# The last sort of a quantile graph layer: operation size and pauses in its DVE sorting network

## The chip, the cores and the metric

The kernel runs on one core of a Trainium2 chip. A core has a matrix engine (TensorE, PE in the profile), a vector engine (VectorE, DVE), a scalar engine (ScalarE, ACT), GpSimd (POOL) and a queue for plain DMAs (SyncE, SP). Each takes its instructions in the order in which they are written and waits for the others by semaphores. The metric is device time in microseconds. Before the change it is 1443.4 us, the median of three runs (1442.67 to 1445.76).

## The reference

For each of 16 graphs of 1024 nodes with 64 features, a layer does the following:

```
h   = max(layernorm(x), 0)
rem = every skip-th neighbour of a node with more than 10, made symmetric
nd  = (adjacency with self loops) without rem
for each node n and each feature c:
    s   = sorted values h[j, c] over the neighbours j of n in nd
    agg = 0.25 * quantile(s, 0.25) + 0.5 * quantile(s, 0.5) + 0.25 * quantile(s, 0.75)
out = h + agg
x   = x + mask * (relu(out @ W1 + b1) @ W2 + b2)
```

A quantile is interpolated between two neighbouring sorted values. The adjacency has about eight neighbours per node, so the lists are short, but they differ in length.

## The kernel before, in words

Two graphs form a pair, so there are eight pairs, m = 0 to 7. Within a graph the nodes are reordered by their number of neighbours and laid out as eight tiles of 128 nodes (tile 0 has the longest lists). For each node the kernel works out a list of neighbour indices. `fetch` (line 1319) then queues one indirect DMA for each slot of each tile and graph, issued by GpSimd at line 1332: it gathers, for 128 nodes, the 64 features of one neighbour into the tile `g`. There are 952 such gathers. In the last pair, `pick` (line 1373) brings some slots by one-hot matmuls instead.

Tiles are sorted in classes of equal slot count: tile 0 (13 slots), tiles 1 to 3 (11), tiles 4 and 5 (9), tiles 6 and 7 (7). The few longest lists of eight graphs are set apart and form a group of rows with a network of its own in the tile `gg` (`set_apart`, line 1483; `fetch_group`, line 1667; `aggregate_group`, line 1694). There are two groups; the second is treated next to the last pair.

`sort` (line 1417) runs a sorting network over the slots, found beforehand and written down in `PLANS`. Each step compares up to a few slots with as many others: a DVE minimum or maximum into a free slot (line 1440) and the opposite, in place (line 1445); a step of which one side only is needed has a single operation (line 1437). Afterwards the slots that can hold a quantile are scaled by their weights: by DVE at line 1462, or, in pairs from the sixth on (`by_act`), by ACT at line 1460, one slot and one node tile at a time. TensorE then sums the scaled slots into `acc` or `gacc` in PSUM (line 1466).

A flag `whole` of `sort` sets how long its operations are and what stands behind them:

```python
        most = max(1, (WHOLE if whole else PART) // size)
        gap = (lambda ins: ins) if whole else opened
```

`PART` is 384 and `WHOLE` is 1024 elements per partition. `size` is the width of one slot: 64 for the group, 128 for tile 0, 384 for tiles 1 to 3, and, in the last pair, 128 for the other two classes, since `aggregate` (line 1496) takes the two graphs of the last pair one after the other there. `opened` (line 856) puts behind an operation a DVE memset of one element of a scratch tile (line 859), called a pause here:

```python
        at = len(tails) % 64
        tails[nc.vector.memset(pause[:, at:at + 1], 0.0).ins.name] = ins.ins.name
        return ins
```

In pairs 0 to 6 and the first group, and in other long DVE operations such as the one-hot comparisons of lines 1392 and 1572, every operation has a pause. In the last pair (`last`) and the second group the sort has `whole` set.

The tail of the program, from about 1286 us, holds the sort of the second group, the MLP of pair 6 (`one_hot`, `sums`, `mlp`), the sort of tile 0, then of tiles 1 to 3, then, graph by graph, of tiles 4 to 7. Before some of these sorts ACT copies a few rows from one tile's slot to another's and DVE overwrites where they stood (lines 1528 and 1531). Results of the group's rows come back into the pair by `bring_back` (line 1726, tile `few`). The MLP of each graph of the last pair follows its sorts; it ends in lines 1615 to 1663.

The order of the instructions on each engine isn't that of the source. `arrange` (line 713) takes the whole list of instructions with their dependences and an assumed cost of each (`Step.cost`: a gather 1345 ns, a DVE operation by its elements, 12 ns more for a pause), plans it forwards and backwards six times, keeps the shortest plan and fixes that order on every engine. A gather may also wait for a DVE or ACT instruction that is planned to end 25 us before it (`LEASH`).

Of the kernel before, what the change touches and what calls it, by code (L numbers as in the profile page):

```python
# [70 lines left out]
GROUP = 8  # L71
# [481 lines left out]
ACTP, ACTB = 5, 13  # L553
# [115 lines left out]
def between(s, o):  # L669

    return s.lag + 60 if o.engine != s.engine or s.moves else 115 if s.engine == "DVE" else 0
# [141 lines left out]
def list_layer(  # L813
# [15 lines left out]
    B = x.shape[0]  # L829
# [489 lines left out]
    def fetch(m, classes=CLASSES, halves=(0, 1)):  # L1319

        for tiles, slots in classes:
            lo, n = tiles[0], len(tiles)
            held, order = PLANS[slots][:2]

            def begin(h, tiles=tiles, lo=lo, n=n, slots=slots, held=held):
                opening((tiles, slots), m)
                nc.scalar.copy(gathered[m, tiles][:, slots - 1, :, h], owns[m][:, lo:lo + n, h])

            issued, given_out = paced

            def gather(h, slot, k, at, tiles=tiles, lo=lo):
                ins = nc.gpsimd.indirect_dma_start(  # L1332
                    out=gathered[m, tiles][:, slot, k - lo, h], out_offset=None, in_=tables[2 * m + h][0],
                    in_offset=bass.IndirectOffsetOnAxis(ap=lists[2 * m + h][:, at:at + 1], axis=0),
                    element_offset=tables[2 * m + h][1], engine_sem=issued,
                )
                given_out[ins.ins.name] = ins
                return ins

            for h in halves:  # L1340
                queue.append(partial(begin, h))
                for k in tiles:
                    for s, slot in enumerate(order[:FULL[k] + ((k, FULL[k]) in HOSTS)]):
                        if m < pairs - 1 or s >= LEAST[k]:
                            queue.append(partial(gather, h, slot, k, PASSED[k] + s))
# [129 lines left out]
    def terms(acc, out):  # L1475

        for n in range(3):
            to = out[n]
            nc.scalar.copy(to, acc)
            if n < 2:  # L1480
                nc.tensor.matmul(acc, minus16, to, start=False, stop=True, skip_group_check=True)  # L1481
# [14 lines left out]
    def aggregate(m, o, between=None):  # L1496


        last = m == pairs - 1
        coef = coefs[m]  # L1500
        for half in (0, 1) if last else (1, 0):
            parts = CLASSES[2 * half:2 * half + 2][::1 if last else -1]
            for sides in ((0, 1), (1, 2)) if last and half else ((0, 2),):
                hs, one = slice(*sides), sides[0] if last and half else None
                if not one:
                    shape = [P, 4, 2, C] if one is None else [P, 2, 4, C]
                    tag, bufs = ("mx", 3) if last and not half else ("agg", 2)
                    whole = psum.tile(shape, F32, name="acc", tag=tag, bufs=bufs)
                    for tiles, slots in parts:
                        rows, own = slice(tiles[0] - 4 * half, tiles[-1] + 1 - 4 * half), gathered[m, tiles][:, slots - 1]  # L1510
                        nc.tensor.matmul(
                            whole[:, rows] if one is None else whole[:, :, rows], ident32,
                            own if one is None else own.rearrange("p n h c -> p h n c"),
                            start=((tiles, slots) == parts[0]), stop=False, skip_group_check=True,
                        )
                acc = whole if one is None else whole[:, one]
                if one is not None:
                    yield from between(one, False)
                line = {}
                for tiles, slots in parts:  # L1520
                    for k in tiles:
                        for s, slot in enumerate(PLANS[slots][1]):
                            line[k, s] = gathered[m, tiles][:, slot, k - tiles[0], hs]
                            if s >= FULL[k] and (k, s) not in HOSTS:
                                nc.vector.memset(line[k, s], BIG)
                for host, guest, first, stop in GUESTS:
                    if host in line:
                        nc.scalar.copy(line[guest][first:stop], line[host][first:stop])
                for host, lo, hi in BARE:
                    if host in line:  # L1530
                        nc.vector.memset(line[host][lo:hi], BIG)
                for tiles, slots in parts:
                    lo, n = tiles[0], len(tiles)
                    g = gathered[m, tiles]
                    plan = PLANS[slots]
                    if one is None:
                        lines, weigh = g.rearrange("p s n h c -> p s (n h c)"), partial(
                            lambda s, many, lo, n: coef[:, s:s + many, lo:lo + n].rearrange("p s n h -> p s (n h)"),
                            lo=lo, n=n,
                        )  # L1540
                    else:
                        lines, weigh = g[:, :, :, one], partial(
                            lambda s, many, lo, n, h: coef[:, s:s + many, lo:lo + n, h], lo=lo, n=n, h=one
                        )
                    yield from sort(
                        lines, plan, window(tiles, slots)[0], weigh, acc[:, lo - 4 * half:lo - 4 * half + n],
                        m >= ACTP, last,
                    )
                    if sides[1] == 2:
                        gathered.pop((m, tiles))  # L1550
                if half and not last:
                    for h in ((0, 1),) if m < pairs - 2 else ((0,), (1,)):
                        fetch(m + 1, CLASSES[2:], halves=h)
                terms(acc, [
                    o[:, 4 * half:4 * half + 4, hs if one is None else one, C * n:C * n + C] for n in range(3)
                ])
                if last and not half:
                    bring_back(m, o)
                if one is not None:
                    yield from between(one, True)  # L1560
# [133 lines left out]
    def aggregate_group(grp):  # L1694
        n = GROUP // 4
        gg = groups.pop(grp)
        to, xg = gathered.pop(("group", grp))
        coef = wk.tile([P, TOP, n], F32, name="gcoef", bufs=1)
        weights(coef, group_num[grp][:, :, 1], n, TOP)
        yield 1.0  # L1700
        tag, bufs = ("mx", 3) if grp == B // GROUP - 1 else ("agg", 2)
        acc = psum.tile([P, n, C], F32, name="gacc", tag=tag, bufs=bufs)
        nc.tensor.matmul(acc, ident32, gg[:, CAP - 1], start=True, stop=False, skip_group_check=True)
        for k in range(n)[::-1]:
            yield from sort(
                gg[:, :, k], PLANS[(CAP, SECOND + 1)[k]], window((0,), CAP)[0],
                lambda s, many: coef[:, s:s + many, k:k + 1], acc[:, k], whole=grp == B // GROUP - 1,
            )
        o = wk.tile([P, n * C], F32, name="go", tag="lows", bufs=1)
        nc.scalar.copy(o, acc.rearrange("p k c -> p (k c)"))  # L1710
        yield 0.0
        tp = psum.tile([P, P], F32, name="ot", tag="misc")
        nc.tensor.transpose(tp, o, ident32)
        ot = wk.tile([P, P], F32, name="got", tag="h1", bufs=1)
        nc.scalar.copy(ot, tp)
        yield 0.0
        h1 = wk.tile([P, n, P], F32, name="gh1", tag="highs", bufs=1)
        for k in range(n):
            hp = psum.tile([P, P], F32, name="hp", tag="misc")
            nc.tensor.matmul(hp, w1[k * C:(k + 1) * C], ot[k * C:(k + 1) * C], start=True, stop=True)  # L1720
            nc.scalar.activation(h1[:, k], hp, AF.Relu, bias=b1c)
            yield 0.0
        output(h1.rearrange("p k r -> p (k r)"), n, group_num.pop(grp)[:, :, 0], xg)
        gathered["out", grp], gathered["sum", grp] = (to, xg), o
# [143 lines left out]
def window(tiles, n):  # L1868

    return min(LEAST[k] for k in tiles) // 4, -(-3 * (n - 1) // 4) + 1  # L1870
# [176 lines left out]
```

## Time and profile before

| | |
|---|---|
| median of three runs | 1443.4 us |
| the profiled execution | 1448.98 us, span 1447.2 us |
| GpSimd busy | 1049.3 us, 73%; its 952 gathers 1013.1 us |
| DVE busy | 1220.1 us, 84% |
| PE busy | 1100.0 us, 76% |
| ACT busy | 1041.4 us, 72% |
| pauses on DVE (line 859) | 2043, the last at 1314.1 us |

The profile is of one execution. Its times are counted from the first instruction. A row of the timeline gives the start and the length in microseconds, the engine, the source line, the operation and its tiles (written<-read), and in brackets how long the engine sat idle before it and what is inferred to have ended that. Instructions of one engine overlap somewhat: a DVE operation's row ends a little after the next one has started, so its cost to the queue is read from start to start. [...]

### The profile page before, as it was taken

How to read it: one execution, taken by the hardware profiler on the slowest of the kernel's cores; microseconds unless marked ns; L12 is line 12 of the kernel's file. 1: busy time of each engine (PE TensorE's matmuls, PEld its weight loads, DVE VectorE, ACT ScalarE, POOL GpSimd, SP SyncE). 2: the span in 40 equal slices, each digit the busy share in tenths (PEclk: the TensorE clock that was granted, in tenths of full speed). 3: DMA queues.
4: the chain of work that ended last, by engine and by line, in shares of the span. 5: the costliest groups of instructions: out<-in, count | busy, mean ns of one | idle time of the engine just before them, and what ended most of it. 6: DMA issues, size and time to landing. Idle time of an engine off the chain costs nothing. (4 is left out here: it accounts for less than half of the span.)

```text
span 1818.2 us, 30222 instructions
## 1 busy us (share of the span) xinstructions
PE 1225.8 (67%) x8995; PEld 774.2 (43%) x9011; DVE 1225.1 (67%) x5869; ACT 1064.3 (59%) x2869; POOL 1028.3 (57%) x991
## 2 busy tenths in 40 slices
PE   6637576578777778567764886646774769623937
PEld 4425344344444445344442544434442446512524
DVE  5605287764786768775658768687657846786895
ACT  7646466567673868356661757363573775324865
POOL 0353565455555656654556565656556656677770
PEclk9759788798888898778887898777896889866958
DMA  5422232222231314121331213231220110112110
GB/s 193 133 77 84 86 96 73 70 68 77 78 112 47 102 37 136 44 74 47 92 98 38 77 44 117 48 94 34 58 72 21 33 24 22 21 25 48 35 26 14
DMA packets 128831, 121.67 MB, mean 67 GB/s; under 512 B 95730, under 2 KB 96274, under 8 KB 128658
## 3 DMA queue, kind: packets, MB, share of 16 engines
q1 hardware_dynamic: 97106, 87.29, 15.6%
q0 software_dynamic: 31552, 32.36, 8.1%
q8 instruction: 73, 1.20, 0.3%
q14 instruction: 100, 0.82, 0.1%
HBM read 108.79 MB, written 9.05 MB: 65 GB/s over the span
## 5 line engine op out<-in xcount | busy, mean ns | idle before, releaser
L1332 POOL DMA_INDIRECT g<-gtab,idx x952 | 991.6, 1042 | 733.5 <-issue 267.7
L1440 DVE TENSOR_TENSOR g<-g 128x384 f32<-128x384 f32 (+2 forms) x659 | 311.5, 493 | 21.6 <-ACT g L1413 7.4
L1445 DVE TENSOR_TENSOR g<-g 128x384 f32<-128x384 f32 (+2 forms) x659 | 310.7, 493 | 10.9 <-DMA gg<-g 6.0
L1145 PE MATMUL codeP<-pack,perm 128*128 128x332 bf16 x1024 | 201.0, 344 | 57.7 <-DVE perm L1120 38.6
L1048 ACT ACTIVATE dist<-rk,bias 128x512 f16<-128x512 f32 x256 | 168.2, 699 | 68.7 <-remote 25.6
L981 ACT ACTIVATE ne<-tp 128x512 fp8e4<-128x512 f32 x248 | 143.3, 610 | 101.4 <-remote 64.0
L1466 PE MATMUL acc<-g,kf 128*128 128x128 f32 (+2 forms) x472 | 148.5, 451 | 71.6 <-ACT g L1460 36.6
L1071 ACT ACTIVATE kept<-kp 128x512 fp8e4<-128x512 f32 x224 | 131.7, 601 | 87.5 <-PE kp L1066 41.8
L968 PE MATMUL tp<-kb,sg 128*128 128x128 bf16 x1024 | 117.7, 249 | 89.4 <-ACT dist L1048 34.2
L1145 PEld LDWEIGHTS <-perm 128*128 128x128 bf16 x1024 | 103.7, 108 | 149.4 <-DVE perm L1120 47.6
L1038 PE MATMUL rk<-kb,cnt 128*128 128x512 bf16 x256 | 114.1, 446 | 72.6 <-ACT dist L1048 38.6
L1043 PEld LDWEIGHTS <-ne 128*128 128x128 fp8e4 x1024 | 91.3, 110 | 132.4 <-issue 109.7
L968 PEld LDWEIGHTS <-sg 128*128 128x128 bf16 x1024 | 88.1, 113 | 127.0 <-issue 107.1
L1460 ACT ACTIVATE g<-g,coef 128x64 f32<-128x64 f32 x336 | 87.7, 341 | 77.0 <-DVE g L1440 65.0
L961 ACT ACTIVATE sg<-at 128x1024 bf16<-128x1024 f32 x122 | 130.6, 1071 | 3.0 <-DMA at<-in_adj_dram 2.8
L1466 PEld LDWEIGHTS acc<-g,kf 128*128 128x128 f32 x472 | 87.9, 225 | 102.8 <-ACT g L1460 46.1
L1049 DVE TENSOR_SCALAR rem<-dist,half 128x1024 bf16<-128x1024 f16 x128 | 62.9, 494 | 98.8 <-ACT dist L1048 88.2
L859 DVE MEMSET pause<- 128x1 bf16 x2043 | 120.5, 59 | 1.8 <-issue 1.8
L1158 ACT CAST st<-codeP 128x4 bf16<-128x4 f32 x128 | 20.7, 162 | 171.8 <-DVE rest L1156 87.3
L1043 PE MATMUL rk<-kw,ne 128*128 128x128 fp8e5 x1024 | 120.8, 245 | 0.0
L1061 PE MATMUL kp<-ne,kw 128*128 128x512 fp8e4 x256 | 108.5, 425 | 18.0 <-ACT kept L1071 9.6
L1066 PE MATMUL kp<-kw,rem 128*128 128x128 fp8e5 x1024 | 111.3, 234 | 0.0
(202 smaller groups left out, 2471.2 us busy)
## 6 DMA issues: line engine op xcount, KB each, us to landing
at<-in_adj_dram SPq DMA_DIRECT2D x122, 512.0 KB
g<-gtab,idx POOLq DMA_INDIRECT x952
xt<-in_x_dram SPq DMA_DIRECT2D x16, 256.0 KB
y<-in_x_dram SPq DMA_DIRECT2D x16, 256.0 KB
gtab<-xt SPq DMA_DIRECT2D x16, 256.0 KB
out_dram<-y SPq DMA_DIRECT2D x14, 256.0 KB
spare<-in_adj_dram SPq DMA_DIRECT2D x6, 512.0 KB
gg<-g SPq DMA_DIRECT2D x32, 48.0 KB
```

What stands on the lines that cost most here:

```text
L859: tails[nc.vector.memset(pause[:, at:at + 1], 0.0).ins.name] = ins.ins.name
L961: nc.scalar.activation(sg, at, AF.Sign)
L968: run.append(nc.tensor.matmul(tp[:, s], sg[:, m * P:(m + 1) * P], ident16, start=(s == 0), stop=(s == 3 and t // 4 != n), skip_group_check ...
L981: nc.scalar.activation(to, tp, AF.Relu, saturate=False)
L1043: run.append(nc.tensor.matmul(rk[:, s * P:(s + 1) * P], ne[:, 4 * n + s, ts], upper, start=False, stop=(s == 3), skip_group_check=True,))
L1048: nc.scalar.activation(dist[:, n * HALF:(n + 1) * HALF], rk, AF.Abs, bias=bias[:, t:t + 1])
L1071: nc.scalar.activation(kept[:, 4 * n:4 * n + 4], kp, AF.Relu, saturate=False)
L1145: run.append(nc.tensor.matmul(flat, perm[:, t, k * P:(k + 1) * P], pack[:, t], start=False, stop=(t == NT - 1), skip_group_check=True,))
L1332: ins = nc.gpsimd.indirect_dma_start(out=gathered[m, tiles][:, slot, k - lo, h], out_offset=None, in_=tables[2 * m + h][0], in_offset=bass ...
L1440: nc.vector.tensor_tensor(at(f + k * df, df, many), pa, pb, OP.min if what == "<" else OP.max)
L1445: nc.vector.tensor_tensor(pa if back else pb, pa, pb, OP.max if what == "<" else OP.min)
L1466: nc.tensor.matmul(acc, ident32, lines[:, s], start=False, stop=(s == now[-1] and not ends), skip_group_check=True)
```

## The change

The flag `whole` is off everywhere. The comparisons of the last pair and of the second group are therefore cut at 384 elements per partition instead of 1024, and each has a pause behind it, as in the pairs before. The order of all engines is worked out anew from the changed list.

```diff
                     yield from sort(
                         lines, plan, window(tiles, slots)[0], weigh, acc[:, lo - 4 * half:lo - 4 * half + n],
-                        m >= ACTP, last,
+                        m >= ACTP, False,
                     )
...
             yield from sort(
                 gg[:, :, k], PLANS[(CAP, SECOND + 1)[k]], window((0,), CAP)[0],
-                lambda s, many: coef[:, s:s + many, k:k + 1], acc[:, k], whole=grp == B // GROUP - 1,
+                lambda s, many: coef[:, s:s + many, k:k + 1], acc[:, k], whole=False,
             )
```

## The prediction

> **What bounds the kernel now.** I read the chain of waits first, for the end of the span:
>
> ```profile
> 1395.99 2.11 POOL g L1332
> ...
> 1398.41 3.84 POOL g L1332
> ...
> 1410.04 2.64 DMA g<-gtab,idx
> ...
> 1412.90 0.76 DVE g L1440 x2
> ...
> 1428.46 2.71 PE acc L1466 x24
> ```
>
> Columns: start, length, what. DVE's last sort (second batch of the last pair, slots of tiles 4 to 7) starts at 1412.9 because a gather issued at 1410.04 has only then landed. GpSimd (POOL) is the queue that is late. Its timeline over the tail shows why:
>
> ```profile
> 1271.02 0.94 POOL L1332 DMA_INDIRECT g<-gtab,idx  x1 [0.30 <-DMA g<-gtab,idx]
> ...
> 1280.28 1.19 POOL L1332 DMA_INDIRECT g<-gtab,idx  x1 [0.30 <-DMA g<-gtab,idx]
> ...
> 1332.45 5.14 POOL L1332 DMA_INDIRECT g<-gtab,idx  x1 [0.30 <-DMA g<-gtab,idx]
> ...
> 1372.01 8.20 POOL L1332 DMA_INDIRECT g<-gtab,idx  x1 [0.30 <-DVE gg L1440]
> 1380.51 0.94 POOL L1332 DMA_INDIRECT g<-gtab,idx  x1 [0.30 <-DMA g<-gtab,idx]
> ```
>
> The idle time before each gather is a constant 0.30 us, so the releasers named there cost nothing: the queue runs back to back, and only the length of a gather varies. Up to 1300 none is longer than 1.62 us; from 1317 on thirteen lie between 1.57 and 8.20. From the one at 1317.51 to the one at 1410.04 there are 50 steps in 92.5 us.
>
> What DVE did beside them is in its timeline:
>
> ```profile
> 1275.29 0.41 DVE L1445 TENSOR_TENSOR g<-g 128x256 f32<-128x256 f32 x1
> 1275.31 0.06 DVE L859 MEMSET pause<- 128x1 bf16 x1
> 1275.63 0.41 DVE L1440 TENSOR_TENSOR g<-g 128x256 f32<-128x256 f32 x1
> ...
> 1336.69 0.42 DVE L1662 TENSOR_TENSOR yp<-yp,mask 128x256 f32<-128x256 f32 x1
> ...
> 1378.42 0.97 DVE L1445 TENSOR_TENSOR g<-g 128x768 f32<-128x768 f32 x1
> 1379.46 0.11 DVE L1531 MEMSET g<- 64x64 f32 x1
> 1379.60 0.96 DVE L1440 TENSOR_TENSOR g<-g 128x768 f32<-128x768 f32 x1
> ```
>
> Around 1275 DVE is as full as later, but each sort operation has a pause behind it, and the eight gathers from 1271.02 to 1281.77 go at 1.344 us each. Without pauses, the long gathers end about 0.8 us after an operation that isn't a comparison of two SBUF tensors: the 8.20 us one at 1380.21, after the memset of 1379.46; the 5.14 us one at 1337.59, after the PSUM operation of 1336.69. So I read the stall as a gather locked out while DVE runs two-input comparisons without a gap. DVE isn't full all along: before the gathers of 1346.98 and 1410.04 it sat idle:
>
> ```profile
> 1349.45 1.01 DVE L1440 TENSOR_TENSOR g<-g 128x768 f32<-128x768 f32 x1 [8.62 <-DMA g<-gtab,idx]
> ...
> 1389.74 0.43 DVE L1440 TENSOR_TENSOR g<-g 128x256 f32<-128x256 f32 x1 [1.68 <-DMA g<-gtab,idx]
> ...
> 1410.63 0.11 DVE L1531 MEMSET g<- 32x64 f32 x1 [9.02 <-ACT g L1528]
> ```
>
> The last is a DMA wait at one remove: ACT's copy in front of that memset waited 9.47 us for a gather. DVE's waits in the tail are POOL's lateness.
>
> **The change part by part.** *Operations, counted from the plans.* Group 1 (rows apart): 142 comparisons and 13 scalings, 64 to 384 elements wide, so none is cut. Last pair: 34 comparisons of tile 0, 35 of tiles 1 to 3, and twice 27 + 17 for tiles 4 to 7. Only tiles 1 to 3 have any above 384: 32 of 768 become 64 of 384. The last pair's scaling is ACT's, one slot at a time, and doesn't change. New: 32 comparisons and 142 + 13 + 34 + 67 + 88 = 344 pauses. No DMA is added.
>
> *A pause.* Its row says 59 ns, but it overlaps. Start to start, ten 256-wide comparisons with pauses from 1275.29 take 3.45 us; ten without from 1415.63 take 3.35. I take 10 ns. [...]
>
> *A cut.* 768-wide steps start 0.87 us apart, 384-wide ones 0.47; with pauses 2 x 0.48 = 0.96 for 0.87. 32 x 0.09 = 2.9 us.
>
> *Sum on DVE.* By stretch: to 1340.9 about 160 pauses, +1.6 us; 1349.4 to 1388.1, 2.9 for cuts and 45 pauses, +3.3; 1389.7 to 1401.7, 36 pauses, +0.4; 1412.9 to 1427.4, 41 pauses, +0.4. In all +5.7 us.
>
> *Gathers.* At 1.344 the 50 steps take 67.2 us: 25.3 less. The gather of 1346.98 (13 steps on) starts at 1335.0 and has landed by 1337.5; that of 1410.04 starts at 1384.7 and lands at 1387.4.
>
> *What is late next.* DVE, with its queue in order. It is through its earlier work at 1340.9 + 1.6 = 1342.5, after the gather has landed, so the sort of tiles 1 to 3 starts at 1342.5 instead of 1349.45 (-6.9). Its stretch to 1388.1 gets +3.3: ends at 1384.5, and the wait of 1.68 goes, so the next stretch starts 5.2 earlier, is 12.0 + 0.4 long and ends at 1396.9. The gather for the last sort landed at 1387.4, 9.5 us earlier, so that gather has that much to spare. The last sort starts at about 1397 instead of 1412.9: -15.9, less 0.4 for its pauses.
>
> *ACT and PE behind it.* ACT's queue holds the copy of 1410.32 and behind it ten scalings that PE waits for at 1411.22 (9.17 us). In front of it are eight scalings ending at 1400.85, released by the stretch that moves by 5. So the copy comes at about 1396, -14.4, and PE's matmuls for the first batch, which fill PE from 1411 to 1428, move by that. This is the smaller of the two, and I take 14 us. The MLP from 1428.5 on is the same work. Against the profiled execution, 1448.98 us with a span of 1447.2, that gives a span of 1433.2 and 1435 us; the median, 1443.4, lies 5.6 below that execution, so 1429.4 us.
>
> [...]
>
> *Order.* The planner works out the order of all engines anew, with 12 ns per pause and 1345 ns per gather; the trace of before can't show the new order. I bound it by 3 us either way.
>
> **Rivals.**
> [...]
> 2. It doesn't do what it does around 1275: the tail's stalls are other than DVE's and stay. Then the 5.3 us of DVE's work before the last gather lie in its idle 8.62 + 1.68 + 9.02 us, and 0.4 us behind it show: 1444. For: at 1303 to 1309, comparisons without pauses ran beside gathers of 0.94 to 1.03. Against: where the long ones end.
> 3. Slower: the pauses don't let gathers in, and DVE's comparisons, cut smaller, fill more time. One more stall like that of 1372.01 costs 8.20 - 0.94 = 7.3 us of the queue that sets the end: 1443.4 + 7 = 1450. It decides from some 3 us more of stalls than the 25.3 now. Against: a pause is a memset, and a memset ended the longest stall.
>
> **How the numbers follow.** Full gain 0.50, its own range 1425 to 1434 (3 us of order, 9.5 us to spare for the gathers); half 0.18 (1432 to 1440); no change 0.10 (1441 to 1446); slower 0.22 (1446.5 to 1456, the price of pauses by the rule at its lower edge). A measurement tells 0.2%, 2.9 us, from no change. Faster 0.68, same 0.10, slower 0.22. The range 1424 to 1450 leaves out half of the slower case and a little below.
>
> **What would show it.** Right: no gather above 1.7 us after 1317, a pause after each comparison to the end at a step of 0.345, 64 comparisons of 384 starting at about 1342, and DVE's waits of 8.62 and 9.02 gone. Wrong: gathers of several us still there; pauses that lengthen the step by far more than 10 ns; or a new wait of DVE for ACT's `few`, which would put the ACT and PE chain in POOL's place.

## The result and the profile after

The kernel with the change takes 1440.74 us, the median of 15 runs (1435.33 to 1444.05); the kernel before took 1443.19 (1437.3 to 1447.63) beside it. The ratio is 0.9983, with an interval from 0.9969 to 0.9996: 2.5 us or 0.17% less, where 14 us or 1% had been forecast. Nearly all of the forecast gain is missing, so the question is where it went.

First the counts. The groups of the page of after:

```profile
L1332 POOL DMA_INDIRECT g<-gtab,idx x952 | 982.7, 1032 | 354.1 <-DMA g<-gtab,idx 152.0
L1440 DVE TENSOR_TENSOR g<-g 128x384 f32<-128x384 f32 (+1 forms) x675 | 312.9, 483 | 3.9 <-ACT g L1413 2.7
...
L859 DVE MEMSET pause<- 128x1 bf16 x2387 | 140.8, 59 | 0.0
```

There are 344 more pauses than the 2043 of before and 16 more minima at line 1440 (675 for 659), as counted. The gathers of line 1332 took 982.7 us of GpSimd for 1013.1, and DVE's idle time before line 1440 fell from 25.3 to 3.9 us. Read alone, these rows would say that the change did what was forecast.

The chain of waits of after (start, length, what; its first row is a gather, from its start to the landing of its data) says otherwise:

```profile
1374.22 2.58 DMA g<-gtab,idx
...
1386.34 8.45 ACT g L1460 x35
...
1397.53 0.29 ACT o L1745
1397.84 0.28 DVE few L1747
...
1403.56 5.49 PE acc L1466 x24
```

The end hangs no longer on a gather for DVE's last sort. It hangs on 35 scalings of ACT, and through them on DVE's addition to `few` (the tile into which the results of the group's rows come back). DVE's timeline has one long wait left in the tail, a new one:

```profile
1336.04 0.15 DVE L1849 TENSOR_SCALAR flag<-fp 1x1 int32<-1x1 f32 x1 [0.37 <-PE fp L1848]
...
1353.05 0.27 DVE L1445 TENSOR_TENSOR gg<-gg 128x128 f32<-128x128 f32 x1
1353.06 0.06 DVE L859 MEMSET pause<- 128x1 bf16 x1
1353.26 0.21 DVE L1437 TENSOR_TENSOR gg<-gg 128x64 f32<-128x64 f32 x1
...
1397.84 0.28 DVE L1747 TENSOR_TENSOR few<-few,o 32x128 f32<-32x128 f32 x1 [9.89 <-ACT o L1745]
```

ACT's timeline shows why `few` is late:

```profile
1384.40 0.24 ACT L1528 COPY g<-g 64x64 f32<-64x64 f32 x1 [8.27 <-DMA g<-gtab,idx]
1384.65 10.13 ACT L1460 ACTIVATE g<-g,coef 128x64 f32<-128x64 f32 x42
1394.69 0.24 ACT L1741 COPY few<-back 32x128 f32<-32x128 f32 x1
...
1397.53 0.28 ACT L1745 CAST o<-few 32x128 bf16<-32x128 f32 x1
```

The copy of line 1528 stood 8.27 us for a gather; behind it in ACT's queue were 42 scalings, and behind those the casts that DVE waits for. So gathers are late again. GpSimd's timeline has the reason:

```profile
1336.78 17.51 POOL L1688 DMA_INDIRECT gx<-in_x_dram,gto  x1 [0.30 <-issue]
1354.60 1.21 POOL L1332 DMA_INDIRECT g<-gtab,idx  x1 [0.30 <-issue]
```

One gather, of the group's own rows of x, took 17.51 us. From its start to the 64-wide comparison of 1353.26, and with that one, 48 comparisons started on DVE, each with a pause behind it. I say of such a gather that it is held. It took longer than any gather of before, where the longest has 8.20 us. It belongs to line 1688, so the row of line 1332 above doesn't contain it. Summed over all indirect DMAs of GpSimd from 1285 us on, the time above 0.94 us each fell only from 32.1 to 24.0 us, and 16.6 of the 24.0 is this one. It ended at 1354.29, 1.03 us after the start of the 64-wide comparison shown.

### The profile page after: what moved, and what is told of

Read it like the earlier page. It is cut to its first block, busy times and chain, and to the rows that moved or that the text cites. A ratio compares the mean times of both kernels' runs of the same rounds, so it can differ in the third digit from the quotient of the medians.

```text
span 1846.1 us, 30586 instructions
## 1 busy us (share of the span) xinstructions
PE 1216.6 (66%) x8994; PEld 759.1 (41%) x9011; DVE 1228.0 (67%) x6245; ACT 1061.0 (57%) x2869; POOL 1022.1 (55%) x991
## 5 line engine op out<-in xcount | busy, mean ns | idle before, releaser
L1440 DVE TENSOR_TENSOR g<-g 128x384 f32<-128x384 f32 (+1 forms) x675 | 314.3, 486 | 19.9 <-remote 13.4
L1445 DVE TENSOR_TENSOR g<-g 128x384 f32<-128x384 f32 (+2 forms) x675 | 312.5, 484 | 5.6 <-PE rk L1043 3.6
L1466 PE MATMUL acc<-g,kf 128*128 128x128 f32 (+2 forms) x472 | 141.0, 434 | 73.9 <-DVE pause L859 28.5
L859 DVE MEMSET pause<- 128x1 bf16 x2387 | 140.8, 59 | 3.0 <-issue 2.8
L1074 PE MATMUL code<-kw,kept 128*128 128x17 fp8e5 x1024 | 65.4, 173 | 74.8 <-ACT kept L1071 42.0
```

What stands on the lines that cost most here:

```text
L1440: nc.vector.tensor_tensor(at(f + k * df, df, many), pa, pb, OP.min if what == "<" else OP.max)
L1445: nc.vector.tensor_tensor(pa if back else pb, pa, pb, OP.max if what == "<" else OP.min)
L1466: nc.tensor.matmul(acc, ident32, lines[:, s], start=False, stop=(s == now[-1] and not ends), skip_group_check=True)
```

## The experiments

The diffs are against the kernel before or after, as said. `silent` and `planned` only decide what cost the planner `arrange` sees. All ratios are to the kernel before on the same chip.

| kernel | median, us (range, runs) | ratio (95%) |
|---|---|---|
| the change again (e1) | 1441.09 (1433.25–1443.46, 22) | 0.9977 (0.9963–0.999) |
| cut, no pauses (e2) | 1447.51 (1435.93–1452.04, 22) | 1.0034 (1.0019–1.0049) |
| every fourth pause wide (e3) | 1433.81 (1431.33–1436.87, 7) | 0.9933 (0.9909–0.9956) |
| pauses alone, order of before (e4) | 1429.03 (1426.37–1429.66, 6) | 0.9903 (0.9876–0.9929) |
| pauses alone, new order (e5) | 1437.25 (1429.59–1446.48, 22) | 0.9957 (0.9937–0.9976) |
| cut and pauses, order of before (e6) | 1430.17 (1428.66–1433.27, 6) | 0.9911 (0.9885–0.9938) |
| wide pauses in the group alone (e11) | 1433.5 (1430.43–1437.55, 6) | 0.9933 (0.9912–0.9953) |
| pauses in the group alone (e12) | 1428.14 (1426.14–1430.29, 4) | 0.9889 (0.9866–0.9912) |
| pauses in the last pair alone (e13) | 1435.01 (1433.65–1436.61, 5) | 0.9944 (0.9925–0.9964) |

**The change again (e1).** The kernel of after, unaltered.

> The changed kernel once more, for a second profile. Theory A (chance): a gather that meets DVE at the wrong moment stays locked out until DVE runs something other than a two-input comparison, so where and how long depends on timing; then the 17.5 us gather of 1336.8 us is not at the same place or not of the same length, and the span moves with it (down to some 1433 us if no gather is longer than 3 us, some 1440 if one is 15 us or more). Theory B (fixed place): the second gather of input rows for the group (line 1688) is slow for a reason of its own; then it takes 15 to 20 us again and the span is within 2 us of 1440.6.

The median, 1441.09, is that of after. The execution that was profiled was one of its few short ones: 1434.64 us with a span of 1432.9; four of the 22 lie below 1437 and 14 at 1440.75 or above. In it, the gather that took 17.51 us takes 1.05. Its GpSimd timeline, and then its DVE timeline:

```profile
1336.35 1.05 POOL L1688 DMA_INDIRECT gx<-in_x_dram,gto  x1 [0.30 <-issue]
```

```profile
1391.40 0.28 DVE L1747 TENSOR_TENSOR few<-few,o 32x128 f32<-32x128 f32 x1 [1.59 <-ACT o L1745]
```

ACT's copy of line 1528 comes at 1377.95 without a wait, the addition to `few` 6.4 us earlier than in after, and the span is 7.7 us shorter. It is the same program on both sides, so I read those 7.7 us as the long gather's. One more run of the same kernel (e7) gave 1431.98 us with a span of 1430.2, again with no long gather (1.24 us). So two profiles of short executions have no long gather, and the only profile of an execution near the median has one; that the other executions near 1441 us have one too is inferred from their times.

> A third profile of the changed kernel. Its times lie between 1433 and 1444 with most near 1441. If one long lock-out is what makes the difference, a run above 1438 has one gather of 8 us or more between 1310 and 1390 us and a DVE wait for few of 5 us or more, and a run below 1436 has neither.

**The cut without the pauses (e2).** Against after; the planner still reckons with 12 ns for each, so the order is that of after.

```diff
-        most = max(1, (WHOLE if whole else PART) // size)
-        gap = (lambda ins: ins) if whole else opened
+        most = max(1, PART // size)
+        gap = (lambda ins: (silent.add(ins.ins.name), ins)[1]) if whole else opened
...
-                        m >= ACTP, False,
+                        m >= ACTP, last,
...
-                lambda s, many: coef[:, s:s + many, k:k + 1], acc[:, k], whole=False,
+                lambda s, many: coef[:, s:s + many, k:k + 1], acc[:, k], whole=grp == B // GROUP - 1,
```

> The changed kernel's order and sizes (384), but no pauses in the last pair and the second group; the planner is told the same costs, so that all engines keep the changed kernel's order. If the pauses are what lets the gathers in: several gathers of 2 to 8 us after 1310 us, their length beyond 0.95 us summing to 20 us or more against some 22 in the changed kernel's profile (16.6 of them one gather), and the time is 1440 to 1448. If size alone does it (a gather waits for at most one operation): no gather above 1.5 us, and 3 us less DVE work, so 1428 to 1436. If neither matters to the end: 1438 to 1442.

It is slower than before, by 0.34%, and slower than after. Against before it has two differences, the cut and the new order, so the 0.34% can't be put down to the cut; against after it lacks only the pauses, which are worth 6.4 us in this order (1447.51 against 1441.09). GpSimd's timeline of e2:

```profile
1318.57 3.53 POOL L1332 DMA_INDIRECT g<-gtab,idx  x1 [0.30 <-DVE gg L1440]
1322.41 9.62 POOL L1332 DMA_INDIRECT g<-gtab,idx  x1 [0.31 <-DMA g<-gtab,idx]
...
1369.55 9.88 POOL L1332 DMA_INDIRECT g<-gtab,idx  x1 [0.30 <-DMA g<-gtab,idx]
```

These two gathers take 9.62 and 9.88 us though none of DVE's operations while they are held lasts longer than 0.54. So a gather isn't held for one instruction of DVE but across many, and with none above 384 elements the holds are no shorter than the 8.20 us of before. The pauses do the work: after has none of these stalls, but one of its own, at a gather of line 1688, and those take 0.97 and 0.95 us in e2.

**The pauses alone, order and sizes of before (e4).** Against before. The pauses are added, the planner isn't told of them, and each engine's order stays as it was.

```diff
-            at.busy += 12
+            at.busy += 0 if tails[ins.name] in silent else 12
...
-        gap = (lambda ins: ins) if whole else opened
+        gap = partial(opened, planned=not whole)
```

> The kernel before, its sizes (up to 768) and its order, with a one-element pause behind each comparison of the last pair and the second group, not counted by the planner. If pauses let the gathers in: the gathers' excess from 1317 us to the end falls from 25 us to 10 or less, DVE's waits for gathers of 8.6 and 9.0 us shrink to under 2, and the time is 1428 to 1436. If pauses do little (only order and size changed anything): 1441 to 1447 with stalls of 3 to 8 us still there.

1429.03 us, 14.4 less than before on its chip (1443.47). Here the gain is whole. From 1285 to 1388 us its longest gathers last 1.73 us; in GpSimd's timeline of e4, and DVE's beside it:

```profile
1341.06 1.73 POOL L1332 DMA_INDIRECT g<-gtab,idx  x1 [0.30 <-ACT at_p L1567]
```

```profile
1341.03 0.94 DVE L1445 TENSOR_TENSOR g<-g 128x768 f32<-128x768 f32 x1
1341.04 0.06 DVE L859 MEMSET pause<- 128x1 bf16 x1
1341.91 0.28 DVE L1440 TENSOR_TENSOR gg<-gg 128x128 f32<-128x128 f32 x1
```

The gather comes just behind the start of a 768-wide comparison and takes 0.79 us more than 0.94: about as long as that comparison keeps DVE, 0.88 us from start to start. With a pause behind each operation, nine of the ten gathers above 1.45 us in this stretch end 0.88 or 0.89 us after the start of DVE's next operation: they wait for the end of the running one and no longer. One indirect write (line 1752, at 1388.30) takes 2.21 us, for 0.93 when it is free, and is held across several comparisons with pauses, so even here a pause doesn't always let the DMA in. The last sort's first comparison starts at 1392.20 instead of 1412.90.

**The change in the order of before (e6).** Against before: e4, and the comparisons cut at 384, both pieces of one at the place of the whole. This is the change without its new order.

```diff
-        most = max(1, (WHOLE if whole else PART) // size)
-        gap = (lambda ins: ins) if whole else opened
+        most = max(1, PART // size)
+        gap = partial(opened, planned=not whole)
...
+        if ins.name in halves: found[ins.name] = join(found[halves[ins.name]], ins); continue
```

> Sizes and pauses as in the changed kernel (at most 384, a one-element pause behind each), but every engine in the order of the kernel before: a cut comparison's two pieces stand where the whole one stood, and neither pieces nor pauses are counted by the planner. DVE's work up by 32 x 0.09 = 2.9 us against pauses alone (1429.0). If the new order is what cost the gain: 1429 to 1434. If the cut does it (384-wide comparisons with pauses can lock a gather out for long): 1437 to 1445, with a gather of 8 us or more.

1430.17 us: 1.1 above e4, with intervals that overlap, so the cut costs about a microsecond or nothing. Against after, which has the same operations and pauses in another order, it is 10.6 us faster. The new order takes the gain away. It isn't that the old order never holds a gather; GpSimd's timeline and then DVE's in e6:

```profile
1337.30 6.49 POOL L1688 DMA_INDIRECT gx<-in_x_dram,gto  x1 [0.30 <-DVE gg L1445]
```

```profile
1342.76 0.21 DVE L1437 TENSOR_TENSOR gg<-gg 128x64 f32<-128x64 f32 x1
```

This one was held 5.5 us, and ended 1.03 us after the start of a 64-wide comparison, as in after. It cost nothing that shows: the span, 1426.9, is the shortest of all the profiles.

**The pauses alone, planned anew (e5).** Against before: `gap = opened`, so the planner sees 12 ns for each pause and arranges the operations of before's sizes as it likes.

> One part of the change alone: pauses behind the comparisons of the last pair and the second group, sizes up to 768 as before, and the planner free to order anew with its 12 ns per pause. If the cut is what lets long lock-outs survive beside pauses: as with pauses in the old order, 1427 to 1432, no gather above 2.3 us. If the new order does it, whatever the sizes: 1438 to 1444, with a gather of 8 us or more in the profile or in most runs.

The median, 1437.25, stands between two clusters: 11 executions from 1429.59 to 1434.61 and 11 from 1439.89 to 1446.48. The profiled one (1433.07) is of the lower, and has no gather above 1.72 us. A new order alone, without any cut, thus costs most of the gain in half of the executions. No profile fell in the upper cluster, so that a held gather is the reason there too isn't shown.

**Every fourth pause wide (e3, e11).** Against after, in its order: every fourth of the new pauses writes 64 elements of four bytes (into another tile, `turned`) instead of one of two, in e3 in all the sorts concerned, in e11 only in the larger network of the second group (25 of them, from 1304.76 to 1338.82 us, earlier than e10's expectation has them). Of the diff only the memset is shown; `longer` is set in those sorts alone.

```diff
-        tails[nc.vector.memset(pause[:, at:at + 1], 0.0).ins.name] = ins.ins.name
+        tails[nc.vector.memset(turned[:, turn4[0] // 4 % 8 * P:][:, :P] if longer and not turn4[0] % 4 else pause[:, at:at + 1], 0.0).ins.name] = ins.ins.name
```

> The changed kernel in the same order; every fourth pause of the last pair's and second group's sorts is a memset of 64 four-byte elements in place of one. DVE work up by some 86 x 0.07 = 6 us. If a wider memset ends a lock-out for certain: no gather above 3 us after 1290, ACT's copy of the guest rows (line 1528) waits under 2 us where it waited 8.3, and DVE's wait for few (9.9 us) falls to 3 or less; time 1430 to 1437. If ACT's and PE's order sets the end whatever the gathers do: 1440 to 1447, with the 9.9 us wait still there.

> [...] The changed kernel with 25 wide pauses in the group's larger network: 1431 to 1437 with no run above 1438 if the usual 1441 comes from a lock-out in that stretch; median 1439 to 1442 if it comes from elsewhere.

1433.81 and 1433.5 us, no run of either above 1437.6, and the longest gather from 1285 us on is 2.00 and 2.01 us in their profiles. In e11 the addition to `few` waits as little as in the short executions of after (DVE's timeline):

```profile
1389.88 0.28 DVE L1747 TENSOR_TENSOR few<-few,o 32x128 f32<-32x128 f32 x1 [1.64 <-ACT o L1745]
```

Its longest gather, on GpSimd, and a wide pause on DVE:

```profile
1336.57 2.01 POOL L1688 DMA_INDIRECT gx<-in_x_dram,gto  x1 [0.30 <-DVE gg L1445]
```

```profile
1337.23 0.11 DVE L859 MEMSET turned<- 128x64 uint32 x1
```

This gather, too, starts just behind the flag operation of line 1849 (1336.10 in e11). It doesn't end 0.88 us after the operation behind the running one has started, as in e4 (that would be 1337.81), but 0.89 us after the start of the second operation behind the wide pause (1337.69). In e3 the like happens to a gather of line 1332, at 1340.18. Only two of e11's 25 wide writes, at 1337.23 and 1338.82, lie within the stretch in which after's gather was held.

With the 25 wider writes the kernel takes 7.2 us less than after (1440.7 to 1433.5). That fits a long gather in most of after's executions, beside the group's larger network, which lifts the median; the wide writes also shift what meets what in time, and no run tells the two apart.

**The pauses in one place only (e12, e13).** Against before, in its order and sizes: in e12 only the second group's 155 operations have pauses, in e13 only the last pair's 157 comparisons. The diff is e12's; e13 has `whole in (0, 1)` instead.

```diff
-        gap = (lambda ins: ins) if whole else opened
+        gap = partial(opened, planned=not whole) if whole in (0, 2) else lambda ins: ins
...
-                lambda s, many: coef[:, s:s + many, k:k + 1], acc[:, k], whole=grp == B // GROUP - 1,
+                lambda s, many: coef[:, s:s + many, k:k + 1], acc[:, k], whole=2 * (grp == B // GROUP - 1),
```

> As e8: the kernel before with pauses behind the second group's operations alone. 1433 to 1439 if each network's own pauses matter; 1442 to 1447 if only the last pair's do.

> As e9: the kernel before with pauses behind the last pair's comparisons alone. 1431 to 1438 if each network's own pauses matter; 1442 to 1447 if only the group's do.

e12: 1428.14 us, the lowest median of all kernels here, and not to be told from e4. e13: 1435.01 us, somewhat more than half the gain. GpSimd's timeline of e13, and its DVE timeline:

```profile
1313.09 3.49 POOL L1332 DMA_INDIRECT g<-gtab,idx  x1 [0.30 <-DVE y L1663]
...
1318.83 4.87 POOL L1332 DMA_INDIRECT g<-gtab,idx  x1 [0.30 <-DMA g<-gtab,idx]
```

```profile
1315.54 0.21 DVE L1437 TENSOR_TENSOR gg<-gg 128x64 f32<-128x64 f32 x1
...
1340.05 0.96 DVE L1440 TENSOR_TENSOR g<-g 128x768 f32<-128x768 f32 x1 [3.65 <-DMA g<-gtab,idx]
```

The stalls beside the group's sort stay, the first of them again until 1.04 us after the start of a 64-wide comparison, and DVE waits 3.65 us for the gathers behind. Pauses in the last pair's own sort add nothing measurable to those in the group's (e4 against e12). An indirect write of line 1752 takes 4.49 us in e12 beside the last pair's sort without pauses, and the time doesn't show it.

The three kernels had been run once before, those of e12, e13 and e11 as e8, e9 and e10, when the kernel before itself took 1831.44 us; all three came within 0.5% of it (1830.76, 1834.3 and 1839.68 us). GpSimd then sat idle 246, 232 and 268 us before the gathers of line 1332 with nothing shown that it waited for, so those runs say nothing of the tail.

> The kernel before, its order and sizes, pauses (not counted by the planner) only behind the second group's operations (155). Pauses behind both gave 1429.0. If a gather gets in at the pauses of whichever network runs beside: the group's run to about 1373 us, so the stalls of 3.5 to 5 us between 1317 and 1338 go (10 to 13 us of them), and those of the last pair alone (1372, 1396, 1398) may stay: 1433 to 1439. If only the last pair's pauses matter: 1442 to 1447.

> The kernel before, its order and sizes, pauses (not counted by the planner) only behind the last pair's comparisons (157). If each network's own pauses matter: the group's stretch from 1317 to 1330 keeps its stalls (8 us), the later ones go: 1431 to 1438. If only the group's pauses matter: 1442 to 1447.

> The changed kernel, its order and sizes; only in the group's larger network (about 1322 to 1364 us, beside the gather that took 17.5 us) every fourth pause, 25 in all, is a memset of 64 four-byte elements. If the changed kernel's usual 1441 comes from a lock-out in that stretch: 1431 to 1437 and no run above 1438. If it comes from elsewhere in the tail, or from the order itself: median 1439 to 1442 as without them.

## Why the prediction was wrong, step by step

**What bounds the kernel** was read rightly. Gathers, held for up to 8.20 us beside DVE's unpaused comparisons, made the last sort late. With pauses and nothing else altered (e4) the gain is 14.4 us; 14 were forecast. That the two agree so well is in part luck: the sum was made on a profile that lay 5.6 us above its median, and from that profile to e4's the span fell by 20.1 us and the start of the last sort by 20.7, for 15.9 forecast.

**The counts and the price of a pause** hold. 344 pauses and 32 comparisons were added. In after, 256-wide comparisons start 0.346 us apart (1379.70 for the first two, then 1380.39 to 1385.93), with 0.335 before without pauses: about 10 ns. DVE's busy time grew by 5.2 us, for 5.7 forecast. The lower edge of the slower case, 1446.5 us, was set by a dearer pause, and no run shows such a price: the runs showed about 10 ns in its place, and e4, with 312 more pauses than before (2355 for 2043), is 14.4 us faster.

**The cut** is 0.96 us for 0.87, as forecast: 384-wide comparisons with pauses start 0.48 apart (1364.09, 1364.57, 1365.05). Of the 2.9 us, about 1.1 or nothing shows at the end (e6 against e4).

**The cut alone** doesn't let the gathers in: e2 has no operation above 384 and no pauses, and gathers are held there for 9.62 and 9.88 us. With pauses, in e4, the gathers of line 1332 from 1285 us on lose at most 0.79 us, about the rest of one 768-wide operation.

**"Gathers at 1.344"** is the first step that failed. It took the pauses as enough to let every gather in, from eight gathers around 1275. In after nearly all go at that pace (1.34 us for the 73 others from 1285 us on, by their excess of 7.4 us), but one was held through 48 comparisons and their pauses and took 17.51 us. The prediction's argument against its rival 3 was that "a memset ended the longest stall". That memset was 64 elements wide; the pause is one element. The long stalls of after and e6 and the first of e13 ended 1.03, 1.03 and 1.04 us after the start of a 64-wide comparison; others ended, as in before, at a memset of 64 elements or an operation on PSUM (the 9.88 us one of e2 0.75 us after the start of the memset of 1378.68, the 4.88 us one of before 0.90 us after that of the PSUM operation of 1327.23), and the 9.62 us one of e2 when DVE had nothing to run (it is idle for 2.08 us up to 1333.28). The prediction had overlooked that in before, too, stalls ended at such comparisons, which have both inputs in SBUF. GpSimd's timeline of before, and DVE's beside it:

```profile
1317.51 3.48 POOL L1332 DMA_INDIRECT g<-gtab,idx  x1 [0.30 <-DVE y L1663]
```

```profile
1319.97 0.21 DVE L1437 TENSOR_TENSOR gg<-gg 128x64 f32<-128x64 f32 x1
```

This is not a sure rule: a 64-wide comparison passed in this very stall (1318.62), in the first of e13 (1314.20) and in the 9.62 us one of e2 (1324.28) and let nothing in. In the order of after, 17.2 us pass between the flag operation, which reads PSUM, and the next 64-wide comparison (1336.04 to 1353.26); between two operations of these kinds there are at most 13 us in before and 14.5 in e6. What it costs follows from the prediction's own spare time: the gathers had 9.5 us in hand, the long one takes 16.6 us more than 0.94, and 7.1 is left; the spans of after and e1 differ by 7.7. (The 9.5 were worked out for the old order, so that the figures agree is partly luck.)

**"Order: I bound it by 3 us either way"** is the second step that failed. The order costs 10.6 us (after against e6). Of these, 7.2 are put down to the long gather, which by the times comes in most executions of the new order (after against e11). The other 3.3 us (e11 against e6, the 25 wide writes included) would be the order proper; the intervals of the two overlap, so this part is uncertain. In the two profiles, whose spans differ by 4.4 us, the difference lies in two places: from the flag of line 1849 to the addition to `few` pass 53.8 us in e11 and 50.7 in e6, and from there to the end 41.4 and 39.4. So 3 us was a fair bound for a tail without stalls; it left out that an order can also decide how long DVE runs without anything that lets a gather in.

**"What is late next"**: it was said that a new wait of DVE for ACT's `few` would show the prediction wrong. It is there, 9.89 us. But it wasn't a chain of ACT and PE in its own right; ACT stood 8.27 us for a gather first. Without the long gather the wait is 1.59 us.

**The rivals.** Half the gain (1432 to 1440) is nearest to the short executions of after, but not because the gathers go slower: in the profiles of e1 and e7 none takes more than 1.33 us from 1285 us on. "It doesn't do what it does around 1275" gave 1444, near the median, and is refuted by e4. Rival 3's mechanism, one more stall, is the one that came. That its price of 7.3 us is near the 7.2 measured is luck: rival 3 meant a stall of that size with nothing to spare, and the one that came was 16.6 us too long with several microseconds in hand. It came on top of a gain that was real, so it took back half of it, and the order some 3 us more. After is neither 7 us above before nor 14 below.

**What stays open.** Why the gather is held in most executions of the new order and let in at once in others isn't settled. In after it starts 0.7 us behind the flag operation of line 1849, the last in front of the 17.2 us. In e3 and e11 a gather starts 0.5 us behind it and is held until just behind a wide pause. In e1 and e7 gathers start at the flag or 1.2 us behind it and take 0.94 to 1.25 us. So the moment behind the flag may decide; these are five profiles, and none was made to test it. In the old order e6's held gather starts 0.5 us behind the flag too, but in e12 and e13 one does and takes 1.19 us. The gathers held in after and e6 are both of line 1688, but e3's is of line 1332, and in e1, e4, e5 and e7 none of line 1688 takes over 1.24 us in this stretch. That the width of an operation is what opens the way, and not its time or what it writes to, is argued from where stalls ended; e3 and e11 changed width and time together. What in the new order makes the tail some 3 us longer wasn't taken apart.

## What to carry to other kernels

When an edit also makes a planner arrange everything anew, predict and measure the two apart: the edit in the old order (here −13 us), then the order (here +11). A bound for an unseen order has to include single long waits (here one gather of 17.51 us), whose cost is not proportional to the change in the plan. And put a remedy only where the stall is: pauses behind the group's 155 operations alone, hidden from the planner, gave the lowest median, 1428.14 us.

## What the runs showed of the hardware

A one-element write behind each comparison mostly lets a gather in at the end of the running one (in the tail of e4, nine of the ten longest of line 1332 end 0.88 or 0.89 us after DVE's next operation starts), but not always: one took 17.51 us through 48 comparisons with their pauses, and with 25 writes of 64 elements around that place none of six runs took more than 1437.55 us. The same program can differ from execution to execution by whether a gather is caught: two executions of after differ in span by 7.7 us, one with the long gather and one without. The spread of the times fits that, though only a few executions were profiled: 10 us in the 22 runs of e1 (1433.25 to 1443.46), two clusters some 10 us apart in the 22 of e5, and 3.3, 4.6 and 4.2 us in the 6, 6 and 4 runs of e4, e6 and e12. A profile of one execution can therefore show the rarer case, as e1's did (1434.64 us, with 18 of its 22 runs above 1437); its span has to be held against the spread of the runs before its rows are taken for the median's.
